# A fourth proj_w product made of seven smaller ones, and the sums of the second operand reordered, in a cross-attention block

## The chip, the cores and the metric

The kernel runs on one core of one Trainium2 chip. The metric is the device time of one execution in microseconds (us). The core has five engines that matter here, each with a queue of its own that it works through in order: TensorE (PE in the profile, its weight loads are PEld), VectorE (DVE), ScalarE (ACT), GpSimd (POOL) and SyncE (SP). In this kernel nearly all data transfers (DMAs) are issued by SP, so a transfer that has to wait also holds up those behind it in SP's queue.

## What is computed

The reference is one transformer block with cross-attention. What matters here is its last part, the MLP on the attention result `hidden` (8 sequences of 256 tokens with 512 features, taken two sequences at a time):

```python
y = layer_norm(hidden, ln2_w, ln2_b)
y = jax.nn.gelu(y @ fc_w + fc_b, approximate=True)   # 512 -> 2048
y = y @ proj_w + proj_b                              # 2048 -> 512
return residual + y
```

All of it is float32. Each float32 matmul stands as two MATMUL records in the profile.

## The kernel before

**Staging.** Four groups (g = 0 to 3) of 512 tokens each go through attention first (until about 350 us of the span) and then, one after another, through the MLP. In the MLP of a group, seven `product` calls make the 512-to-2048 part (k = 0 to 6; each is itself seven small products of four 128-column matmuls), then GELU runs on ACT, and then the 2048-to-512 part follows, which is what the change touches.

**Strassen's seven products.** The 2048-to-512 part multiplies h (512 tokens by 2048) by proj_w (2048 by 512), both cut into 2 by 2 blocks. Winograd's form of Strassen's scheme needs seven block products instead of eight, at the price of sums of blocks. The sums of h are called s1 to s4 and those of proj_w t1, t2, t4; the seven products are (11, 11), (s3, 12), (12, 21), (s2, t2), (s1, t1), (s4, 22) and (22, t4), in the kernel's order. `A_SUMS` and `B_SUMS` hold the four sums of each side; within a table each sum after the first needs an earlier one.

**Plain or deep.** `proj` makes one such product with 16 matmuls of 256 columns. From group 1 on (`deep = g > 0`) three of the seven, (s2, t2), (s1, t1) and (s4, 22), are made by `deep_proj` instead: Strassen once more, so seven products of four 128-column matmuls (28 in all). Each of the seven is one call of `sub`. Between them ACT copies and DVE adds the partial results (x1, x2, x3 and the four quarters of r); `deep_proj` also takes small lists of other work (`others`) that it puts into DVE's queue between its own adds. `h_blocks` gives the four h-side sums of one deep product as pieces on DVE; `p2_sums` makes the four proj_w-side sums of one deep product on DVE.

**The store of the proj_w sums.** The proj_w-side sums of a deep product (three blocks of 128 by 512, 768 KB) live in a buffer `p2` with two places (0 and 3). In the kernel before, T1 (t1) holds place 3 for good; T2 (t2) and B22 (22) share place 0. So B22's sums are made once, in group 1, and stored to DRAM (`p2_dram`, L1175); then T2's sums are made in the same place and stored as well; and in each later use `p2_load` (L1188) brings back the one that is needed. Who writes a place waits for the store or the matmuls that still read it.

**The order.** There is no scheduler: `manual_schedule` keeps each engine's instructions in the order in which the program gives them. Around the change this order is written out by hand. The generator `p2_late` makes B22's and T2's sums in group 1: `product` takes one step of it (`next(p2_rest)`) after the first small product of each k, so the sums stand in DVE's queue between the adds that TensorE needs (`add` at L1122 reads a PSUM bank, and the bank is free for TensorE only after that).

**What sits at the end of a group.** In group 0, which makes all seven products plainly, DVE also makes the t sums of proj_w (`some_pw`), T1's sums (`p2_sums("t1")`), the four sums of the next group's y (`y_sums`) and their second-level sums (`split_y`, L307); the adds into the result tile `resm` (`o_add`) stand between them. In groups 1 to 3 DVE makes, in this order: s3 and s2 of h, `u1` from the first product's bank, the pieces of (s2, t2), s1 of h, the pieces of (s1, t1); then the adds of the deep products. POOL makes s4 of h (in place in h12) once (12, 21) has been read. In groups 1 and 2 `turn_next` puts four transposes of the next group's tokens, two at a time, between the products on TensorE.

Of the kernel before, what the change touches and what calls it, by code (L numbers as in the profile page):

```python
# [10 lines left out]
F32 = mybir.dt.float32  # L11
# [5 lines left out]
P = 128  # L17
# [5 lines left out]
def tile_xattn_block(  # L23
# [299 lines left out]
    with ExitStack() as att:  # L323
# [282 lines left out]
        def by_tiles(row):  # L606
            return row[:, None, :].to_broadcast([P, 2, S])
# [352 lines left out]
        g = 1  # L960
# [34 lines left out]
        def run(pieces):  # L995
            for p in pieces:
                p()
# [103 lines left out]
    with ExitStack() as mlp:  # L1101
# [19 lines left out]
        def add(eng, to, a, b, op=ALU.add):  # L1121
            eng.tensor_tensor(to, a, b, op)  # L1122
# [4 lines left out]
        def load_pw(*which):  # L1127
            for n in which:
                f, d = (int(n[0]) - 1) * HF, (int(n[1]) - 1) * HD2
                nc.sync.dma_start(  # L1130
                    pw[n], proj_w.rearrange("(c p) n -> p c n", p=P)[:, f : f + HF, d : d + HD2]
                )
# [16 lines left out]

        p2, p2_at = [], {"t2": 0, "22": 0, "t1": 3}
        p2_dram = {n: tc.dram_tile([P, 3 * S * 2], F32, name=f"p2_dram_{n}") for n in ("t2", "22")}

        def p2_place(n):
            if not p2:
# [13 lines left out]
        def p2_sums(n):  # L1170
            x = pw_blocks(n)
            for i in range(4):
                sum_up(V, x, B_SUMS, i)
                if i == 3 and n != "t1":
                    nc.sync.dma_start(p2_dram[n], p2_place(n))  # L1175
                yield

        def p2_late():

            for n in ("22", "t2"):  # L1180
                for i, _ in enumerate(p2_sums(n)):
                    if n == "t2" or i:
                        yield

        p2_rest = p2_late()

# [10 lines left out]
        for g in range(NG):  # L1197
# [18 lines left out]
            def sum_h(which, q, eng=GP):  # L1216

                x = {n: h[n][:, :, 2 * q : 2 * q + 2, :] for n in h}
                to, a, b, op = {
                    "s3": ("s3", "11", "21", ALU.subtract),  # L1220
                    "s2": ("21", "22", "s3", ALU.subtract),
                    "s1": ("11", "21", "11", ALU.add),
                    "s4": ("12", "12", "21", ALU.subtract),
                }[which]
                add(eng, x[to], x[a], x[b], op)
# [29 lines left out]
            def some_gelus(n=3):  # L1255
                for f in gelus[:n]:
                    f()
                del gelus[:n]
# [17 lines left out]
            def product(k, *sums):  # L1276


                wt, yn = w2[g, k], QI[FC_ORDER[k][1]]
                bank = {}  # L1280

                def y_of(n):
                    if n in QUARTERS:
                        return ys[g].t[:, yn, int(n[0]) - 1, ts(int(n[1]) - 1, P)]
                    return y2s[g][:, ("t1", "t2", "t4").index(n), yn, :]

                def sub(n, w, b, first, last):
                    if first:
                        bank[n] = bank_of(n, f"pf{n}_{k}").rearrange("p i (j s) -> p (i j) s", j=2)
                    for m in range(HF // 2):  # L1290
                        mm(
                            bank[n][:, m, :],
                            wt[:, QI[w], ts(m, P)],
                            y_of(b),
                            first and m == 0,
                            last,
                        )

                def u(n):
                    return us(n, f"u{n}_{k}").rearrange("p i (j s) -> p (i j) s", j=2)  # L1300

                def made(cd, n, x):
                    some_gelus()
                    if k in (3, 4) and cd != "22":
                        norm_piece()
                    if sums[0][1] is None:
                        add(V, block(sums[0][0], cd), bank[n], x)
                        return

                    r = h["s3"][:, parts[0] % 4 // 2, parts[0] % 2 * HF // 2 :][:, : HF // 2]  # L1310
                    parts[0] += 1
                    add(V, r, bank[n], x)
                    for to, base in sums:
                        add(GP, block(to, cd), block(base, cd), r)

                sub(1, "11", "11", True, False)
                u1 = u(1)
                nc.scalar.copy(u1, bank[1])  # L1318
                if g == 1:
                    next(p2_rest)  # L1320
                sub(6, "s2", "t2", True, True)
                u2 = u(2)
                add(V, u2, bank[6], u1)
                some_gelus()
                sub(7, "s3", "12", True, False)
                u3 = u(3)
                add(V, u3, bank[7], u2)
                some_gelus()
                sub(5, "21", "t1", True, False)
                made("22", 5, u3)  # L1330
                sub(1, "12", "21", False, True)
                some_gelus()
                for to, base in sums:
                    if base:
                        add(V, block(to, "11"), bank[1], block(base, "11"))
                    else:
                        nc.scalar.copy(block(to, "11"), bank[1])
                sub(7, "22", "t4", False, True)
                made("21", 7, u2)
                sub(5, "s4", "22", False, True)  # L1340
                made("12", 5, u2)
                load_w2(w2_place[g, k])
# [13 lines left out]
            product(4, ("22", "12"), ("21", "21"))  # L1356
            if g == 0:
                load_pw("21")
            product(5, ("21", "21"))
            norm_piece()  # L1360
            gelu("21", 0)
# [18 lines left out]
            def proj(bank, a, w, first, last, tiles=(0, 1)):  # L1380
                for i in tiles:
                    for p in range(HF):
                        mm(
                            bank[:, i, :] if last_7 is None or i == 0 or bank is not last_7[0] else last_7[1],
                            h[a][:, i, p, :],
                            pw[w][:, p, :],
                            first and p == 0 and (i == 0 or last_7 is not None and bank is last_7[0]),
                            last and p == HF - 1,
                        )
# [11 lines left out]
            def o_add(eng, b, k, x):  # L1401
                o = out_quarter(b, k)
                add(eng, o, x, o)

            u1, u2, u3 = (us(n, f"v{n}") for n in (1, 2, 3))
            proj(bank[1], "11", "11", True, False)
            add(V, u1, bank[1], by_tiles(projb[:, HD2:]))
            some_gelus(HF)
            normalise_next()
            if deep:  # L1410
# [4 lines left out]
            def free(i):  # L1415

                return h["s3"][:, i // 2, i % 2 * HF // 2 :][:, : HF // 2]
# [48 lines left out]
            def as_tiles(r):  # L1466

                return r.rearrange("p c s -> p (c s)").rearrange("p (i s) -> p i s", i=2)
# [3 lines left out]
                run(pieces)  # L1472
            for q in range(NQF):
                sum_h("s1", q, V if deep else GP)
            proj(bank[7], "s3", "12", True, False)
            if deep:
                x_s1, pieces = h_blocks("11", free(0), free(1), free(2))
                run(pieces)
            turn_next(0)
            turn_next(1)  # L1480
            some_pw(4)
            proj(bank[1], "12", "21", False, True)
            o_add(V, 0, 0, bank[1])
            for q in range(NQF):
                sum_h("s4", q)
            turn_next(2)
# [22 lines left out]
            if deep:  # L1509
                x_s4, pieces = h_blocks("12", hsum[:, 0], hsum[:, 1], hsum[:, 3])  # L1510
                run(pieces[:1])
                deep_proj(
                    x_s1, "t1", free(3), pieces[1:2], pieces[2:3], pieces[3:], y_sums[:1], y_sums[1:2]
                )
                for b in range(2):
                    o_add(GP, b, 1, as_tiles(free(3)))
                add_us()
                deep_proj(x_s4, "22", hsum[:, 4], y_sums[2:3], y_sums[3:])
                if g + 1 < NG:
                    p2_load("t2")  # L1520
                o_add(V if g + 1 == NG else GP, 0, 1, as_tiles(hsum[:, 4]))
            else:
                add_us()
                some_pw(4)
                proj(bank[5], "11", "t1", True, True)
                o_add(V, 0, 1, bank[5])
                o_add(V, 1, 1, bank[5])
                for _ in p2_sums("t1"):
                    pass
                run(y_sums)  # L1530
                bank[3] = bank_of(1, "py3")
                proj(bank[3], "12", "22", True, True)
                o_add(V, 0, 1, bank[3])
# [56 lines left out]
```

## Time and profile before

| what | us |
|---|---|
| median of 3 runs (730.57 to 732.4) | 731.34 |
| the profiled execution's own time | 733.88 |
| its span, first to last instruction | 732.1 |
| TensorE busy in the span | 719.0 |
| DVE busy | 488.5 |
| POOL busy | 474.6 |
| ACT busy | 326.4 |
| group 1, from its first product to the GELU part | 52.33 |
| the same in groups 2 and 3, each | 43.77 |

TensorE is busy for 98% of the span, so the table is read from TensorE: a change gains what it takes out of TensorE's work or out of its few idle stretches, and loses what makes TensorE wait. Times within the execution are in us from the start of the span. In group 1 the last part runs from 496.89 to 545.69, in group 2 from 589.46 to 638.27, in group 3 from 682.04 to the end.

### The profile page before, as it was taken

Reading aid. Unit: us, or ns where it says so; the run is one execution under the profiler, and the core shown is the slowest. Engines: PE = TensorE matmul, PEld = TensorE weight load, DVE = VectorE, ACT = ScalarE, POOL = GpSimd, SP = SyncE. Lnnn points to the kernel's source line nnn. Section 1 sums busy time; section 2 is a strip of 40 time slices with the busy share of each in tenths; the row PEclk is TensorE's granted clock in tenths of the full one; section 3 lists DMA queues with packets and bytes.
Section 4 is the critical chain, followed back from the end, with each engine's and each line's share of the span. In section 5 each row is a group of like instructions: output and inputs, shape, how many; then the busy total and the mean of one; then the engine's idle time right before and its main releaser. Section 6 shows DMA issues by size and latency. Waiting matters only on the chain.

```text
span 732.1 us, 14659 instructions
## 1 busy us (share of the span) xinstructions
PE 719.0 (98%) x5325; PEld 633.5 (87%) x5325; DVE 488.5 (67%) x1177; ACT 326.4 (45%) x922; POOL 474.6 (65%) x423
## 2 busy tenths in 40 slices
PE   8999999999999999999999999699999999999998
PEld 7888777887888778777999889699999999999997
DVE  2676765675557557879588587589566894667852
ACT  2268688767777778871226200207103061030500
POOL 3758699987786999876569940475244752437423
PEclk9999999999999999999999999899999999999999
DMA  9515646687648775932899304966127951266011
GB/s 297 174 66 170 247 159 225 197 308 258 218 142 294 273 254 212 357 103 87 290 407 369 141 1 166 351 232 216 44 101 296 333 190 44 84 251 227 1 45 57
DMA packets 76392, 144.37 MB, mean 197 GB/s; under 512 B 7028, under 2 KB 45216, under 8 KB 73632
## 3 DMA queue, kind: packets, MB, share of 16 engines
q1 hardware_dynamic: 76064, 143.42, 55.9%
q8 instruction: 42, 0.69, 0.4%
q14 instruction: 30, 0.25, 0.1%
q0 software_dynamic: 256, 0.02, 0.0%
HBM read 108.29 MB, written 35.13 MB: 196 GB/s over the span
## 4 chain that ended last, share of the span: by engine, by line
PE 93%; DMA 2%; ACT 1%; DVE 1%; issue 1%; POOL 1%; SPq 0%; DVEq 0%; ACTq 0%; POOLq 0%
PE pf L1119 22%; PE py L1119 17%; PE ppt L699 8%; PE pv L441 7%; PE pqT L441 7%; PE po L441 6%; PE pd_t L1119 5%; PE pkT L441 5%; PE s L646 5%; PE av L715 4%; PE pd L1119 3%; PE pkT L538 2%; DMA p_dram<-p 2%; PE pxt L274 1%; PE pyt L274 1%
## 5 line engine op out<-in xcount | busy, mean ns | idle before, releaser
L1119 PE MATMUL pf<-y,w 128*128 128x128 f32 x1568 | 178.4, 277 | 5.9 <-DVE u L1122 5.9
L1119 PEld LDWEIGHTS pf<-y,w 128*128 128x128 f32 x1568 | 178.0, 194 | 6.4 <-DVE u L1122 6.1
L1122 POOL TENSOR_TENSOR h<-h,hs 128x512 f32<-128x512 f32 x88 | 113.5, 1312 | 104.1 <-DVE hs L1122 103.7
L688 POOL TENSOR_TENSOR pr<-pr,rsum 128x512 f32<-128x512 f32 x128 | 129.5, 1044 | 35.2 <-DVE rsum L686 23.4
L674 ACT ACTIVATE pr<-pr,nmax 128x256 f32<-128x256 f32 x256 | 127.6, 502 | 35.5 <-DVE nmax L664 35.3
L664 DVE CUSTOM_DVE_ANT_0 pr<-s,mb 128x256 f32<-128x256 f32 x256 | 93.5, 413 | 39.4 <-PE s L646 27.2
L1318 ACT COPY u<-pf 128x512 f32<-128x512 f32 x28 | 16.4, 585 | 173.0 <-PE pf L1119 173.0
L699 PEld LDWEIGHTS ppt<-ident,pr 128*128 128x128 f32 x512 | 57.3, 140 | 14.9 <-issue 5.6
L699 PE MATMUL ppt<-ident,pr 128*128 128x128 f32 x512 | 68.8, 276 | 0.3
L1119 PE MATMUL py<-pw,h 128*128 128x256 f32 x288 | 63.6, 379 | 0.0
L1119 PEld LDWEIGHTS py<-pw,h 128*128 128x128 f32 x288 | 54.2, 190 | 7.1
L1122 DVE TENSOR_TENSOR hs<-pf,u 128x512 f32<-128x512 f32 x72 | 49.5, 688 | 12.8 <-PE pf L1119 11.7
L1262 ACT ACTIVATE h<-h,cols 128x256 f32<-128x256 f32 x128 | 52.0, 495 | 11.6 <-POOL h L1122 11.6
L1122 DVE TENSOR_TENSOR u<-pf,u 128x512 f32<-128x512 f32 x56 | 38.7, 691 | 25.0 <-PE pf L1119 21.2
L704 ACT COPY pt<-ppt 128x512 f32<-128x512 f32 x96 | 51.7, 573 | 7.1 <-PE ppt L699 7.1
L441 PE MATMUL pv<-vw,ctxT 128*128 128x256 f32 x224 | 52.4, 380 | 0.0
L1122 POOL TENSOR_TENSOR h<-h,h 128x512 f32<-128x512 f32 x20 | 26.5, 1358 | 39.1 <-PE py L1119 39.1
L441 PE MATMUL pqT<-xnT,qw 128*128 128x256 f32 x224 | 51.0, 379 | 0.0
L674 ACT ACTIVATION_READ_ACCUMULATOR pr<-pr,nmax 128x1 f32 x256 | 48.8, 191 | 0.0
L441 PEld LDWEIGHTS pqT<-xnT,qw 128*128 128x128 f32 x224 | 41.4, 190 | 5.0
L441 PEld LDWEIGHTS pv<-vw,ctxT 128*128 128x128 f32 x224 | 41.0, 190 | 5.4 <-issue 0.3
L1119 PE MATMUL py<-pw_t,h 128*128 128x256 f32 x192 | 42.3, 379 | 0.0
(195 smaller groups left out, 1222.3 us busy)
## 6 DMA issues: line engine op xcount, KB each, us to landing
w<-w_dram SPq DMA_DIRECT2D x16, 1792.0 KB, 9.3
w<-in_L_xattn_fc_w_dram SPq DMA_DIRECT2D x36, 256.0 KB, 5.3
w<-w_dram SPq DMA_DIRECT2D x12, 768.0 KB, 7.2
ctx<-in_ctx_dram SPq DMA_DIRECT2D x16, 256.0 KB, 5.3
x<-in_x_dram SPq DMA_DIRECT2D x16, 256.0 KB, 4.9
v_dram<-st_v SPq DMA_DIRECT2D x16, 256.0 KB, 2.3
v<-v_dram SPq DMA_DIRECT2D x16, 256.0 KB, 5.0
resx<-in_x_dram SPq DMA_DIRECT2D x16, 256.0 KB, 4.1
```

The source lines that it names most:

```text
L441: nc.tensor.matmul(bank[n][:, i, :], l[:, c, ts(i, P)], r[:, c, :], start=first and i == 0 and c == 0, stop=last and c == HC - 1, skip_gro ...
L646: nc.tensor.matmul(banks[j][:, i, :], qT[j * HD : (j + 1) * HD, b * S + i * P : b * S + (i + 1) * P], kT[j * HD : (j + 1) * HD, b * SK : ( ...
L664: nc.vector.tensor_tensor_reduce(pr[:, j, i, :], banks[j][:, i, :], mbias[g][1][:, b, :], scale=-SCALE, scalar=FLT_MAX, op0=ALU.add, op1=A ...
L674: nc.scalar.activation(pr[:, j, i, :], pr[:, j, i, :], AF.Exp, bias=nmax[:, j, i : i + 1], scale=-1.0, accum_out=sums[:, j, i : i + 1],)
L688: nc.gpsimd.tensor_tensor(pr[:, j], pr[:, j], rsum[:, j, :, None].to_broadcast([P, NQ, SK]), ALU.mult,)
L699: nc.tensor.transpose(ps[:, kc, ts(i, P)], probs[n][:, j, i, ts(kc, P)], ident)
L704: nc.scalar.copy(pt, ps)
L715: nc.tensor.matmul(av[j * HD : (j + 1) * HD, :], vs[g, hg][:, b * NK + kc, ts(j, HD)], pts[n, j][:, kc, :], start=(kc == 0), stop=(kc == N ...
L1119: nc.tensor.matmul(ps, lhsT, rhs, start=first, stop=last, skip_group_check=True)
L1122: eng.tensor_tensor(to, a, b, op)
L1262: nc.scalar.activation(h[n][:, :, p, :], h[n][:, :, p, :], AF.Gelu_apprx_tanh, bias=col(c_fcb, half * HF + p), scale=1.0,)
L1318: nc.scalar.copy(u1, bank[1])
```

## The change

Five things change, all in the MLP:

1. The product (12, 21) is made by `deep_proj` in groups 1 to 3. Its h-side pieces go into the four quarters of the `hs3` tile (`free(0)` to `free(3)`), and the result into `hsum[:, 4]`. The first product's bank is added to the result directly after `u1` is made, and the pieces of (s1, t1) are made after the new product instead of before it.
2. B21 gets proj_w-side sums like the other three. They are made in group 0 in place 3, stored, and T1's sums then take the same place 3 and are stored too. So place 3 is shared now: B21's sums are loaded in group 1 after product 4 and, in groups 1 and 2, after (s1, t1); T1's are loaded after (12, 21) in groups 1 to 3. That adds two stores and six loads of 768 KB.
3. `p2_late` has two empty steps between the store of B22's sums and T2's first sum, which so falls into product 5 instead of product 3. T2's last two sums and its store come out of an eighth step, ahead of (s3, 12) in the program.
4. In (s4, 22) the last two of the four `y_sums` stand one place later in DVE's queue each.
5. The result of (s4, 22) goes to `free(0)` instead of `hsum[:, 4]`.

```diff
-        p2, p2_at = [], {"t2": 0, "22": 0, "t1": 3}
-        p2_dram = {... for n in ("t2", "22")}
+        p2, p2_at = [], {"t2": 0, "22": 0, "t1": 3, "21": 3}
+        p2_dram = {... for n in p2_at}
...
-                if i == 3 and n != "t1":
+                if i == 3:
                     nc.sync.dma_start(p2_dram[n], p2_place(n))
                 yield
...
         def p2_late():
-            for n in ("22", "t2"):
-                for i, _ in enumerate(p2_sums(n)):
-                    if n == "t2" or i:
-                        yield
+            for i, _ in enumerate(p2_sums("22")):
+                if i:
+                    yield
+            yield
+            yield
+            for i, _ in enumerate(p2_sums("t2")):
+                if i < 2:
+                    yield
+            yield
...
             if g == 0:
                 load_pw("21")
+            if g == 1:
+                p2_load("21")
             product(5, ("21", "21"))
...
-            proj(bank[1], "11", "11", True, False)
+            proj(bank[1], "11", "11", True, deep)
             add(V, u1, bank[1], by_tiles(projb[:, HD2:]))
+            if deep:
+                o_add(V, 0, 0, bank[1])
...
                 sum_h("s1", q, V if deep else GP)
+            if g == 1:
+                next(p2_rest)
             proj(bank[7], "s3", "12", True, False)
-            if deep:
-                x_s1, pieces = h_blocks("11", free(0), free(1), free(2))
-                run(pieces)
             turn_next(0)
             turn_next(1)
             some_pw(4)
-            proj(bank[1], "12", "21", False, True)
-            o_add(V, 0, 0, bank[1])
+            if deep:
+                x_12, pieces = h_blocks("12", *(free(i) for i in range(4)))
+                run(pieces[:2])
+                deep_proj(x_12, "21", hsum[:, 4], pieces[2:3], pieces[3:])
+                p2_load("t1")
+                o_add(V, 0, 0, as_tiles(hsum[:, 4]))
+                x_s1, pieces = h_blocks("11", free(0), free(1), free(2))
+                run(pieces)
+            else:
+                proj(bank[1], "12", "21", False, True)
+                o_add(V, 0, 0, bank[1])
             for q in range(NQF):
                 sum_h("s4", q)
...
                     x_s1, "t1", free(3), pieces[1:2], pieces[2:3], pieces[3:], y_sums[:1], y_sums[1:2]
                 )
+                if g + 1 < NG:
+                    p2_load("21")
...
-                deep_proj(x_s4, "22", hsum[:, 4], y_sums[2:3], y_sums[3:])
+                deep_proj(x_s4, "22", free(0), (), (), y_sums[2:3], y_sums[3:])
                 if g + 1 < NG:
                     p2_load("t2")
-                o_add(V if g + 1 == NG else GP, 0, 1, as_tiles(hsum[:, 4]))
+                o_add(V if g + 1 == NG else GP, 0, 1, as_tiles(free(0)))
             else:
                 add_us()
                 some_pw(4)
+                for _ in p2_sums("21"):
+                    pass
                 proj(bank[5], "11", "t1", True, True)
```

More of the change, by code (lines that the diff above doesn't have):

```diff
@@ L1147, in tile_xattn_block @@
         pw_sums = sum_pw()
-        p2, p2_at = [], {"t2": 0, "22": 0, "t1": 3}
-        p2_dram = {n: tc.dram_tile([P, 3 * S * 2], F32, name=f"p2_dram_{n}") for n in ("t2", "22")}
+        p2, p2_at = [], {"t2": 0, "22": 0, "t1": 3, "21": 3}
+        p2_dram = {n: tc.dram_tile([P, 3 * S * 2], F32, name=f"p2_dram_{n}") for n in p2_at}
         def p2_place(n):
```

## Prediction

> **What bounds the kernel now.** The first view is the busy time of each engine: PE is busy 719.0 of 732.1 us (98%), so only PE's own work and its few idle stretches can move the time. The second is the list of who waited: PE's longest wait is 5.9 us for DVE (u, L1122), then 0.8 us in two (pd for hsum). The third is PE by stretches, from a group's first product to its GELU part, in groups 1, 2 and 3:
>
> ```profile
> core 0: us, PE busy (x), PEclk, DMA share, GB/s
> 444.56:496.89 52.33, 46.41 (x394) 0.93 0.73 263
> 545.69:589.46 43.77, 43.77 (x394) 1.00 0.84 300
> 638.27:682.04 43.77, 43.77 (x394) 1.00 0.56 205
> ```
>
> The same 394 records take 8.56 us more in group 1: 5.92 of it idle, the rest at a lower granted clock (0.93). The chain of waits says where it begins:
>
> ```profile
> 457.95 1.02 DVE p L219
> 458.99 12.71 DMA p_dram<-p
> 471.69 0.02 issue
> 471.72 0.03 DVE p L219
> ...
> 473.86 23.19 PE pf L1119 x184
> ```
>
> DVE ended B22's last sum at 458.97; the store took 12.71 us among big loads; T2's first sum wants the same place and stood at the head of DVE's queue for 7.4 us, and the adds that free PE's banks stood behind it. The clock by microsecond shows the second part of the price:
>
> ```profile
> 471.00:472.00 1.00, 0.00 (x0) 0.81 1.02 436
> 472.00:473.00 1.00, 0.00 (x0) 0.50 1.04 444
> ...
> 477.00:478.00 1.00, 1.00 (x7) 0.50 0.00 0
> 478.00:479.00 1.00, 1.00 (x9) 0.77 0.28 57
> ```
>
> PE stopped at 467.95; the clock halved at about 471.6 and came back at about 478.5, 4.6 us after PE had resumed at 473.86.
>
> **T2's sums moved: -8.56 us.** T2's first sum goes from product 3 to product 5, which starts at 444.56 + 5 x 6.25 = 475.8; the store lands at 471.7, so 4 us to spare. DVE's place in product 3 becomes free, and group 1 should take 43.77 like the others. What is late next: product 5's weights, issued at 463.51, landed 12.5 us later (476.0), 0.2 us after 475.8; so far the stall hid that. With 0.1 for the restart I take +0.3 (0 to 1.5). Product 4's weights (issued 457.25, 9.3 us) land at 466.6 against 469.6.
>
> **The matmuls: -1.98 us.** (12, 21) as plain product is 16 matmuls, 6.91 us in the chain. The existing deep ones take 12.51 us for 112 records, 0.893 us per small product; seven are 6.25. Three groups gain 0.66 each, if fed. Set against each other instruction by instruction, the two programs differ on DVE by 34 more (four sums in group 0; per group four pieces, five adds of partial results, one more add into the result), on ACT by two copies per group, on POOL by none. ACT's copies are hidden: ACT is idle from 507.6 to 511.3 and waits for PE from then on; late, they would delay x2 by 0.27 each. POOL's s4 sums begin near the end of the new product, as they do near the end of the plain one; they are needed at (s4, 22), over 8 us later.
>
> **Feeding it: +7.94 us.** Here the order on DVE against PE decides. Group 1, DVE and then PE:
>
> ```profile
> 506.87 0.68 DVE L1122 TENSOR_TENSOR v<-py,projb 128x512 f32<-128x512 f32 x1
> 507.47 0.68 DVE L1122 TENSOR_TENSOR hsum<-h 128x512 f32<-128x512 f32 x1
> ...
> 512.53 0.68 DVE L1122 TENSOR_TENSOR hs<-h 128x512 f32<-128x512 f32 x1
> 513.31 0.69 DVE L1122 TENSOR_TENSOR hs<-h,hs 128x512 f32<-128x512 f32 x1
> ```
>
> ```profile
> 503.80 7.07 PE L1119 MATMUL py<-pw,hs 128*128 128x256 f32 x32
> 510.70 1.04 PE L274 MATMUL pyt<-ident,hm 128*128 128x128 f32 x8
> 511.57 7.07 PE L1119 MATMUL py<-pw,h 128*128 128x256 f32 x32
> ```
>
> The new product's first small one (11, 11) needs no sum and runs from 511.57 to 512.46. Its second needs the second piece (s2). On DVE that piece stands where the second `hs` of (s1, t1) stands now (513.31 to 514.00), but behind one more add (`o_add` of the first bank, 0.61 from issue to issue, as at 444.82) and, in group 1, behind two T2 sums (0.60 each). So it ends at 514.00 + 1.81 = 515.81, and with 0.04 for the handover PE stands for 3.39 us. Group 2: piece now ends 606.08, + 0.61 + 0.04 = 606.73, against PE at 604.15 + 0.89 = 605.04: 1.69. Group 3 has no transposes to cover it: 698.66 + 0.65 = 699.31 against 695.86 + 0.89 = 696.75: 2.56. Each restart costs 0.1 more (the small product after the hsum wait took 1.00 instead of 0.89). Sum 7.64 + 0.30. Nothing hides this: the GELU and POOL's adds are done by then, and POOL is idle, so DVE runs at its 0.6 us rate.
>
> **Inside it: +1.02 and +0.5 us.** The fourth small product needs the s1 piece, which DVE takes only after adding x2. By the spacing after the hsum stall (bank added 1.20 after the small product's start, next DVE start 0.2 later, 0.68 long) it is ready 2.13 us after the second small one starts; PE wants it at 1.89. With the restart 0.34, three times. The pieces of (s1, t1) now stand between this product and the adds of (s2, t2): `o_add` and four pieces, some 3.8 us with POOL's s4 sums alongside (DVE's adds took 1.4 instead of 0.6 us while POOL added, at 498.84). In groups 1 and 2 two transposes cover it; in group 3 x3 of (s2, t2) comes some 0.4 us late: +0.5 (0 to 1). The loads of T1's sums have 9 us and took 4.1 to 4.4.
>
> **Group 0's end: +1.5 us.** T1's sums now wait for the store of B21's. The DVE rows there:
>
> ```profile
> 432.22 0.68 DVE L219 TENSOR_TENSOR p<-pw_t 128x512 f32<-128x512 f32 x1
> ...
> 437.85 0.69 DVE L1122 TENSOR_TENSOR resm<-py,resm 128x512 f32<-128x512 f32 x1 [0.42 <-PE py L1119]
> ...
> 441.58 1.08 DVE L307 TENSOR_TENSOR y<-y,y 128x896 f32<-128x896 f32 x1
> 444.82 0.69 DVE L1122 TENSOR_TENSOR resm<-py,resm 128x512 f32<-128x512 f32 x1 [2.16 <-PE py L1119]
> ```
>
> B21's four sums (2.6 us, as T1's) start at 430.5 and end at 433.1. Hardly a transfer runs there; 768 KB stores of other tiles took 4.0 (cw), 4.2, 5.0 and 6.5 us (w), the two of p_dram 8.6 and 12.7 among loads. I take 4.0, for the quiet. T1's sums start at 437.15 instead of 432.22; behind them stand the y sums, an add, `split_y` and the add that frees bank 7. That add would end at 437.15 + 2.53 + 2.6 + 0.61 + 4.1 + 0.69 = 447.7; PE wants the bank at 444.56 + 2 x 0.893 = 446.35: 1.4 and a restart. Each us more of the store is one more of waiting: +2.5 at 5.0, +4.0 at 6.5, +6.1 at 8.6; 0 if it took 2.6, near the 2.2 of a 256 KB store.
>
> **y sums later: -1.32 us.** From the start of (s2, t2) to that of (22, t4) groups 1 and 2 need 19.42 and 19.43 us, group 3, without y sums, 18.76. The y sums stood ahead of the add that the seventh small product waits for; moved behind, DVE still ends `split_y` before the next group's second small product. Writing to the hs3 tile takes no DVE or PE time: its last readers are a product earlier. The other five loads and one store go into SP stretches with no transfers (GB/s near 0 from 506 to 524); what hides them is that quiet, and one that came late would cost its lateness.
>
> **Sum.** -8.56 + 0.3 - 1.98 + 7.94 + 1.02 + 0.5 + 1.5 - 1.32 = -0.60 us. The profiled execution took 733.88 (span 732.1, 1.8 around it), so 733.3; the median of the runs is 2.5 lower, and from it the forecast is 731.34 - 0.6 = 730.7.
>
> **A rule against it.** The trace has one long stop: the clock halved 3.65 us after PE stopped, and that cost 8.56 - 5.92 = 2.64. My largest new stop is 3.39, so I price no clock loss; no row shows a stop of 1 to 5 us, so each may cost 0 to 2.64. The Trainium skill ("TensorE: Matmul & The Clock Gate", section "HAM oscillation — how this bites in real kernels") says that idle gaps over about 3.4 us throttle the clock to half, by a free-running window; the 3.65 agrees. By that rule taken to the letter 3.39 stays just under and the sum stands at 730.7; with the gap a little longer, or nearly a window counted as one, the sum would be 733.3.
>
> **Rivals.**
> - *The clock falls in the new stops* (slower). PE stands 3.4 and 2.6 us before the new product's second small one in groups 1 and 3; if a mostly idle stretch is enough, each costs 2.64: 730.7 + 5.3 = 736.0. It decides from about 2.6 us of idleness. For: the clock did fall here. Against: it took 3.65 us. 0.13.
> - *The covers hold* (faster). The store of B21 is covered, product 5's weights come in time, group 3's x3 too: -1.5 - 0.3 - 0.5, so 728.4, less if the second pieces come sooner than the rows say. For: each is a margin of under 1.5 us. Against: DVE's queue is in strict order and its spacings come from rows. 0.27.
> - *B21's store takes 8.6 us* as T2's did among loads: PE stands 6 us at group 1's start, + 4.6 and a clock fall of 2.6: 737.9. Against: hardly a transfer runs from 426 to 438. 0.08.
> - *It doesn't do what it says*: B22's store still lands after T2's first sum in product 5, the stall stays: 739.3. It would have to land 4 us later. 0.02.
>
> **Chances.** Forecast 0.50 (own range 729.1 to 733.5). About 0.3% (2.2 us) is what a measurement can tell from no change; so faster 0.27, same 0.50, slower 0.23. The range leaves out the two last rivals and the far end of the second: 727.5 to 736.0.
>
> **What would show it.** In the changed profile: group 1's seven products at 44 to 45 us with clock 1.00 and no p_dram wait on the chain (T2 step); PE waits for DVE hs of about 3.4, 1.7 and 2.6 us at pd (feeding), with clock 1.00 through them (no fall); a DVE wait for p_dram near 434 and PE waiting 1.4 us in group 1's first product; 18.8 us from (s2, t2) to (22, t4) in groups 1 and 2. The forecast is wrong if the pd waits are under 1 us, or the clock drops beside them.

## The result and the profile after

The changed kernel takes **733.8 us** (median of 20 runs, 732.06 to 738.58), the kernel before 731.77 (20 runs beside them, 730.57 to 733.71). The ratio is 1.0031 with a 95% interval of 1.0018 to 1.0043: 2.0 us slower, where the forecast was 0.6 faster. The profiled execution took 734.65 with a span of 732.9.

PE by stretches in the changed kernel: first the seven products of group 1, then the last parts of groups 1, 2 and 3. The columns are length, PE busy with its records, granted clock, DMA share and GB/s.

```profile
442.90:487.98 45.08, 44.35 (x394) 1.00 0.85 327
...
487.98:540.43 52.45, 49.46 (x338) 0.97 0.37 132
584.21:634.47 50.26, 48.25 (x339) 1.00 0.34 122
678.24:732.90 54.66, 48.06 (x322) 0.97 0.14 49
```

Group 1's products have fallen from 52.33 to 45.08, at full clock: the stop for T2's first sum is gone. All three last parts have grown, and in groups 1 and 3 the clock there is 0.97.

| stretch | before | after | forecast of the difference | measured |
|---|---|---|---|---|
| group 1, products | 52.33 | 45.08 | -6.76 | -7.25 |
| group 1, last part | 48.80 | 52.45 | +2.51 | +3.65 |
| group 2, last part | 48.81 | 50.26 | +0.81 | +1.45 |
| group 3, last part to the end | 50.06 | 54.66 | +2.84 | +4.60 |
| sum | | | -0.60 | +2.45 |

The two profiled spans differ by only 0.8 us, because the profiled execution of the kernel before reached the first of these stretches 1.66 us later (at 444.56 against 442.90); a second profile of the same kernel reached it at 441.64.

The list of who waited has a new wait at its head (us in total, times, longest); the old one, 5.9 us for DVE's u, is no longer there:

```profile
PE pd L1119 <- DVE hs L1122: 7.2, 4, 3.0
```

The new product's small products in group 1, on PE's timeline (start, length; x8 is one small product; the bracket gives the idle time before it and its releaser):

```profile
502.67 1.06 PE L1119 MATMUL pd<-pw,h 128*128 128x128 f32 x8
506.71 1.16 PE L1119 MATMUL pd<-p,hs 128*128 128x128 f32 x8 [2.99 <-DVE hs L1122]
507.70 1.62 PE L1119 MATMUL pd<-pw,hs 128*128 128x128 f32 x8
509.11 1.95 PE L1119 MATMUL pd<-p,hs 128*128 128x128 f32 x8
510.85 1.34 PE L1119 MATMUL pd<-pw,h 128*128 128x128 f32 x8
```

A fed small product starts 0.893 after the one before. Here the second starts 4.04 after the first (the stop: 3.15 lost), and then come starts 0.99, 1.41, 1.74 and 1.18 apart (the next one is at 512.03): the last three have no listed wait and are slow. The clock says why (half-microsecond slices; PEclk is the number after the records):

```profile
506.50:507.00 0.50, 0.29 (x2) 1.00 0.94 393
...
507.50:508.00 0.50, 0.50 (x7) 1.00 0.94 369
508.00:508.50 0.50, 0.50 (x5) 0.53 0.01 0
...
511.00:511.50 0.50, 0.50 (x5) 0.56 0.00 0
```

The clock halved at 508.03 (a slice at 0.53 is full speed for 0.03 us), 1.3 us after PE had resumed, and came back at 511.44. The stops before the same small product in groups 2 and 3 are shorter:

```profile
601.52 1.16 PE L1119 MATMUL pd<-p,hs 128*128 128x128 f32 x8 [1.57 <-DVE hs L1122]
...
695.54 1.91 PE L1119 MATMUL pd<-p,hs 128*128 128x128 f32 x8 [2.44 <-DVE hs L1122]
```

Group 3's clock falls too, from 695.76 to 699.17; group 2, with the shortest stop, keeps its clock.

```profile
695.50:696.00 0.50, 0.46 (x3) 0.76 0.00 0
...
699.00:699.50 0.50, 0.50 (x5) 0.83 0.00 0
```

### The profile page after: what moved, and what is told of

It reads as the page before. It is cut to its first block, busy times and chain, and to the rows that moved or that the text cites. A ratio compares the mean times of both kernels' runs of the same rounds, so it can differ in the third digit from the quotient of the medians.

```text
span 732.9 us, 14878 instructions
## 1 busy us (share of the span) xinstructions
PE 718.0 (98%) x5397; PEld 634.3 (87%) x5397; DVE 509.9 (70%) x1211; ACT 327.7 (45%) x928; POOL 477.4 (65%) x423
## 4 chain that ended last, share of the span: by engine, by line
PE 77%; DVE 9%; DMA 6%; issue 4%; ACT 2%; POOL 1%; SPq 0%; DVEq 0%; POOLq 0%
PE pf L1119 19%; PE ppt L699 8%; PE pv L441 7%; PE pqT L441 7%; PE py L1119 5%; PE pd L1119 5%; PE po L441 5%; PE pkT L441 5%; PE s L646 5%; PE av L715 4%; PE pd_t L1119 4%; PE pkT L538 2%; DVE h L1122 2%; DMA pw<-in_L_xattn_proj_w_dram 2%; DMA w<-w_dram 2%
## 5 line engine op out<-in xcount | busy, mean ns | idle before, releaser
L1119 PEld LDWEIGHTS pf<-y,w 128*128 128x128 f32 x1568 | 175.9, 192 | 1.3 <-DVE resm L1122 0.7
L1119 PE MATMUL pf<-y,w 128*128 128x128 f32 x1568 | 176.3, 275 | 0.7 <-DVE resm L1122 0.5
L1122 POOL TENSOR_TENSOR h<-h,h 128x512 f32<-128x512 f32 x20 | 28.0, 1425 | 43.7 <-DVE hs L1122 42.8
L1119 PE MATMUL py<-pw,h 128*128 128x256 f32 x192 | 42.4, 379 | 0.0
L1119 PEld LDWEIGHTS py<-pw_t,h 128*128 128x128 f32 x192 | 36.2, 190 | 4.7
```

The costliest lines, as they stand in the source:

```text
L1119: nc.tensor.matmul(ps, lhsT, rhs, start=first, stop=last, skip_group_check=True)
```

## The experiments

All were run beside the kernel before, which took 731.93 us (first four) and 732.08 (last four). The question of the first four: is the rest of the price the clock, and is the gain of T2's move what I took it to be?

**The kernel before again, with a new profile.** No edit.

> The kernel before, unchanged, for its granted clock run by run. Clock theory (the missing 2.6 us are lost because the clock falls in the changed kernel's new stops of PE): nothing special is expected, its stop of 5.9 us costs a clock fall in nearly every run, mean clock about 0.995 as in the profile. Rival (the profiled execution of the kernel before was dear, 733.9 against a median of 731.8, because it paid a clock fall that most of its runs don't, so that moving T2's sums gains only about 6 us in the median instead of 8.56): mean clocks of 0.998 to 1.0 in most runs, with times of 731 to 732 there and 733 to 734 at 0.995.

732.27 us (730.85 to 732.7, 11 runs); PE's stop is 5.83 us long and the clock is between 0.993 and 0.995 in every run. So the kernel before pays for its stop each time, and the rival falls. This profile's span is 729.1 against 732.1 of the one that I predicted from.

**T2's move alone.** In the kernel before, only the new `p2_late`, and its last step ahead of (s3, 12):

```diff
+            if g == 1:
+                next(p2_rest)
             proj(bank[7], "s3", "12", True, False)
```

> Of the change only T2's sums moved behind B22's store; the product (12, 21) stays plain. Clock theory: the whole 8.56 minus 0.3 for product 5's weights is gained in the median too: 731.8 - 8.3 = 723.5. Rival: only the idle time and its restart, 6.0 minus 0.3: 726.1. Both: group 1's seven products at about 44 us, clock 1.00, PE waits for DVE under 1.5 us in all.

723.14 us (722.87 to 724.58), ratio 0.9883 (0.9869 to 0.9896), clock 0.999 to 1.000: 8.8 us gained. Group 1's products in its profile, against 52.33 at a clock of 0.93:

```profile
442.30:486.33 44.03, 44.03 (x393) 1.00 0.83 313
```

Both the idle time and the clock's share come back. It follows that the rest of the change costs 733.8 - 731.77 + 8.8 = 10.8 us.

**PE kept busy in the new stops.** The changed kernel, with transposes into a scratch bank in front of the second small product of (12, 21):

```diff
+                if fill:
+                    warm_ps = ps_m.tile([P, G], F32, tag="mm", name=f"keep_{g}")
+                    for k in range(fill):
+                        nc.tensor.transpose(warm_ps[:, ts(k % NT, P)], ident, ident)
                 sub(1, "s2", "t2", True, True)
...
-                deep_proj(x_12, "21", hsum[:, 4], pieces[2:3], pieces[3:])
+                deep_proj(x_12, "21", hsum[:, 4], pieces[2:3], pieces[3:], fill=(0, 13, 7, 11)[g])
```

> The changed kernel with transposes of the identity that nobody reads put on PE between the first and the second small product of (12, 21), 13, 7 and 11 of them in groups 1 to 3 (2.9, 1.6 and 2.5 us), so that PE is busy while it waits for the second piece; the waiting itself stays. Clock theory: the clock stays at 1.00 there, each fall that is avoided gives 1.6 us, and with two falls in most runs the median drops by 2 to 3.3: 730.5 to 731.8. Rival: the stops are what costs, not the clock: 733.8, within 0.5.

733.02 us (732.09 to 734.76), ratio 1.0015 (1.0007 to 1.0024), clock 0.998 to 1.000: between the two expectations. PE's waits in its group 3:

```profile
694.02 1.16 PE L1119 MATMUL pd<-p,hs 128*128 128x128 f32 x8 [1.24 <-DVE hs L1122]
696.32 1.13 PE L1119 MATMUL pd<-p,hs 128*128 128x128 f32 x8 [0.25 <-DVE hs L1122]
705.67 1.16 PE L1119 MATMUL pd_t<-p,h 128*128 128x128 f32 x8 [1.07 <-DVE p L1122]
```

The profile's clock is 1.00 throughout the last parts, so the falls came from PE's idleness in the stops. But two waits that the slow clock had covered appear: 0.25 for the s1 piece (0 in the changed kernel's group 3) and 1.07 for x2 or x3 of (s2, t2) (0.68 there). The last part of group 1 went from 52.45 to 51.69 and of group 3 from 54.66 to 53.89: by these two stretches a fall costs 0.77 net, not the 1.6 that its slow small products lose. The transposes took 0.11 each, so 13 of them filled only 1.4 us of group 1's stop.

**The pieces first.** The changed kernel with the pieces of s2 ahead of the s1 sums and of T2's last sums, which go between the new product's own adds:

```diff
-            for q in range(NQF):
-                sum_h("s1", q, V if deep else GP)
-            if g == 1:
-                next(p2_rest)
+            s1_sums = [lambda q=q: sum_h("s1", q, V if deep else GP) for q in range(NQF)]
+            if not deep:
+                run(s1_sums)
...
-                deep_proj(x_12, "21", hsum[:, 4], pieces[2:3], pieces[3:])
+                deep_proj(x_12, "21", hsum[:, 4], pieces[2:3], pieces[3:], s1_sums[:2], s1_sums[2:])
+                if g == 1:
+                    next(p2_rest)
...
-                x_s1, pieces = h_blocks("11", free(0), free(1), free(2))
-                run(pieces)
+                x_s1, s1_pieces = h_blocks("11", free(0), free(1), free(2))
...
-                deep_proj(x_s2, "t2", hsum[:, 4])
+                deep_proj(x_s2, "t2", hsum[:, 4], *([f] for f in s1_pieces))
```

> The changed kernel with DVE's order altered: the first two pieces of (12, 21) ahead of the four s1 sums and of T2's last sums; these follow inside the new product, and the pieces of (s1, t1) inside (s2, t2). Both theories: the stops of 3.15, 1.73 and 2.60 us before the second small product shrink to 0, 0 and about 0.2, and the late x2 and x3 of (s2, t2) go. Clock theory: 7.3 of stops, 1.2 of late adds and 2.8 of clock: 733.8 - 11.3 = 722.5. Rival: without the clock's share: 725.3.

727.96 us (727.7 to 729.96), ratio 0.9954 (0.994 to 0.9967), clock 1.000. The long stops are gone, down to 0.25 each, and yet the kernel is 4.8 us behind T2's move alone. On DVE in group 1:

```profile
506.11 2.65 DVE L1122 TENSOR_TENSOR h<-h,h 128x512 f32<-128x512 f32 x2
...
508.89 3.23 DVE L1122 TENSOR_TENSOR h<-h,h 128x512 f32<-128x512 f32 x2
```

Two s1 sums took 2.65 and 3.23 us, because POOL added s4 at the same time (from 504.76, four adds in 6.82); in the changed kernel, ahead of POOL's, four took 2.49. PE then waited 1.77 for T2's last sums (512.25 to 513.45) and 1.17 for the load of T1's, and in group 3 1.15 for an add of a partial result (hsum). Both expectations (722.5 and 725.3) fell: the sums moved away from one stop came back as others. The Trainium skill ("SBUF — State Buffer", section "SBUF: two separate sides") says that a VectorE operation with two SBUF inputs and a GpSimd operation take turns at a shared port; that agrees in kind, and the price here is 1.3 to 1.6 us for an add instead of 0.6.

The question of the last four: how much of the price goes with the product itself, and does a better order exist?

**T2's move and the y sums, without the product.** T2's move alone, and:

```diff
-                deep_proj(x_s4, "22", hsum[:, 4], y_sums[2:3], y_sums[3:])
+                deep_proj(x_s4, "22", free(0), (), (), y_sums[2:3], y_sums[3:])
...
-                o_add(V if g + 1 == NG else GP, 0, 1, as_tiles(hsum[:, 4]))
+                o_add(V if g + 1 == NG else GP, 0, 1, as_tiles(free(0)))
```

> The run with T2's sums alone moved, and with it the parts of the change on the y sums and on where the result of (s4, 22) goes; (12, 21) stays plain. My step: 0.66 in each of groups 1 and 2, so 1.3 below that run's 723.1: 721.8, and 18.8 us from (s2, t2) to (22, t4) in groups 1 and 2. Rival (DVE catches the y sums up elsewhere, at the next group's first product): 723.1.

**722.15 us** (722.0 to 722.18), ratio 0.9861 (0.9841 to 0.9881). This version beats both kernels. Group 1's products take 44.03, and its last parts 48.14, 48.14 and 50.05; those of groups 1 and 2 stand against 48.81 with T2's move alone: the y sums are worth 0.67 twice, as forecast. Through all of group 2, from its products at 534.83 to its last one at 619.83, the chain of waits is PE and nothing else:

```profile
534.83 43.77 PE pf L1119 x392
578.60 13.82 PE py L1119 x64
...
601.07 12.51 PE pd_t L1119 x112
613.58 6.25 PE pd L1119 x56
619.83 6.91 PE py L1119 x32
```

**The fourth product without its h-side sums.** The changed kernel; the four sums are left out and stale data stands in for them:

```diff
-                x_12, pieces = h_blocks("12", *(free(i) for i in range(4)))
-                run(pieces[:2])
-                deep_proj(x_12, "21", hsum[:, 4], pieces[2:3], pieces[3:])
+                x_12, pieces = h_blocks("12", *(hsum[:, i] for i in range(4)))
+                deep_proj(x_12, "21", hsum[:, 4])
```

> The changed kernel without the four h-side sums of (12, 21): its small products read sums of another product, so this part of the result is not what it should be; the matmuls, the partial adds, loads and stores stay. If the pieces on DVE are what the new product costs, its stops go (3.15, 1.73 and 2.60 us, 0.3 in the middle, the clock falls and the late adds of (s2, t2)), and it gains its 0.66 per group against plain: 721.8 of the run before this one, less 2.0, plus 1.1 at group 0's end: 720.9. Rival (the seven small products are dearer than 6.25 us even when fed, or the loads and partial adds cost): 722 to 725 with 6.5 to 7.5 us for the product.

723.48 us (722.69 to 723.9), ratio 0.9879 (0.9861 to 0.9896): the rival's 722 to 725, by its second condition, since the seven small products take 6.25 us where they are fed. By stretches (group 1's products and group 2's last part):

```profile
442.47:487.62 45.15, 44.33 (x393) 1.00 0.86 328
...
579.87:627.44 47.57, 47.57 (x339) 1.00 0.35 126
```

In group 2 PE never waits, and the seven small products gain 0.57 (47.57 against 48.14): the gain of the matmuls exists. But group 1's products still pay 1.1 (45.15 against 44.03) for B21's store and the late weights, and PE waits for adds of partial results, 0.63 in group 1 (behind T2's last sums, 1.76 each beside POOL) and 0.68 in group 3. Its slowest run is faster than any of the changed kernel, its fastest slower than any without the product. Part of that is of this edit's own making: with nothing on DVE reading h12 any more, POOL starts s4 at 503.17 instead of 509.03 and slows T2's last sums (0.68 each in the changed kernel), and the wait behind them costs 0.9 of the 1.3 us that this version lies above the one without the product. So even with its h-side sums free the product would gain nothing clear here.

**The product with T2 where it was.** The changed kernel with the old `p2_late`, no eighth step.

> The changed kernel with T2's sums put back to product 3. If the parts add up, the stall behind the store is back at 8.6 less 0.3: 733.8 + 8.3 = 742.1. Rival (part of that gain depends on the other parts, because stops in one place give transfers time elsewhere): 739 to 741.

740.97 us (739.87 to 741.13), ratio 1.0116 (1.0097 to 1.0134). That is 8.9 over the kernel before, 6.9 more than the changed kernel's 2.0: T2's move is worth 6.9 beside the product and 8.8 alone, the rival's side. With T2's last two sums out of its way the piece of s2 came 0.9 us sooner in group 1, and group 3 kept its clock (53.89 against 54.66), which together make 1.7 of the 1.9 between them. PE's stops in groups 1 and 3, and then the last parts around them with their clock:

```profile
512.68 1.53 PE L1119 MATMUL pd<-p,hs 128*128 128x128 f32 x8 [2.08 <-DVE hs L1122]
...
701.53 1.16 PE L1119 MATMUL pd<-p,hs 128*128 128x128 f32 x8 [2.45 <-DVE hs L1122]
```

```profile
494.85:546.39 51.54, 49.46 (x338) 0.97 0.35 135
...
684.21:738.10 53.89, 46.66 (x322) 1.00 0.14 50
```

Two falls begin in this execution, one in the old stall (468.94) and one at the stop of 2.08 us (513.32 to 516.72):

```profile
468.50:469.00 0.50, 0.00 (x0) 0.94 1.05 446
```

```profile
513.00:514.00 1.00, 1.00 (x8) 0.66 0.00 0
...
516.00:517.00 1.00, 1.00 (x8) 0.64 0.00 0
```

The stop of 2.08 us had its clock halved and the stop of 2.45 did not: length alone does not decide.

**Another order.** The pieces first (`s1_sums` and `s1_pieces` are lists as in the run above), T2's sums two to a step inside the products, and the s1 sums between the adds of (s2, t2):

```diff
-                if i < 2:
+                if i % 2:
                     yield
-            yield
...
-                deep_proj(x_s2, "t2", hsum[:, 4])
+                deep_proj(x_s2, "t2", hsum[:, 4], s1_sums[:2], s1_sums[2:], s1_pieces[:1], s1_pieces[1:3], s1_pieces[3:])
```

> The run with the pieces first, with DVE's work spread further: T2's sums two to a step in products 5 and 6, the s1 sums and the pieces of (s1, t1) inside (s2, t2), nothing but its own pieces inside (12, 21). If DVE's order is the whole trouble, the 1.8, 1.2 and 1.2 us that PE still waited in (s2, t2) go, and (12, 21) gains its 0.66 per group: 728.0 less 5 to 6: 722 to 723, at or just under the run that moves T2's sums alone. Rival (DVE has too much work between a group's GELU and (s1, t1), however it is ordered): above 724.5.

726.95 us (726.11 to 727.35), ratio 0.9926 (0.991 to 0.9941), clock 1.000. T2's sums pushed DVE past PE within group 1's products:

```profile
480.08 6.52 PE L1119 MATMUL pf<-y,w 128*128 128x128 f32 x56 [0.81 <-DVE u L1122]
487.17 2.05 PE L1119 MATMUL pf<-y,w 128*128 128x128 f32 x16 [0.57 <-DVE u L1122]
```

Those products take 47.30 against 44.03 without the fourth product. And group 2, which has no T2 sums, still takes 48.41 against 48.14: waits of 0.25 and 0.17, with what PE loses around them, take 0.84 (48.41 against the fed 47.57). The time lies on the rival's side (above 724.5), but most of the excess is T2's sums inside the products (47.30 against 44.03), not the place that the rival names. No order that was tried gains anything from the product.

## Why the prediction was wrong

**T2's sums moved (-8.56, with +0.3 for product 5's weights) and y sums (-1.32): right.** Together -9.58; the version with these two alone measured 722.15 - 732.08 = -9.93. Its group 1 products took 0.26 more than 43.77, lost where product 5 begins; in the changed kernel the listed wait for these weights is 0.25.

**The matmuls (-1.98): right to a seventh.** 0.57 a group in the one fed case, forecast 0.66.

**Feeding it: the stops were right.** Listed waits of 2.99, 1.57 and 2.44. Against a fed start, the second small product lost 3.15, 1.74 and 2.60, where 3.39, 1.69 and 2.56 were forecast. The restarts cost 0.1, as taken.

**A rule against it: the step that failed.** "My largest new stop is 3.39, so I price no clock loss." The clock fell in groups 1 and 3 after stops of 3.0 and 2.4 us, and the next small products lost 0.52 + 0.85 + 0.29 = 1.66 (group 1) and 0.82 + 0.81 + 0.12 = 1.75 (group 3). The forecast had 0.34 in these places for the s1 wait, and in group 3 the restart's 0.1 as well; so +1.3 in each group. I had read the 3.65 us from stop to fall in the old stall as the shortest stop that costs a fall. It is one delay, and says nothing of shorter stops. (Nor is it so that no row showed a stop of 1 to 5 us: the list of waits has one of 1.4 at the very start; it has no bearing on these.)

The rival that named this had the mechanism, at 0.13; its price of 5.3 was too high. The 2.64 was carried over from a fall that lasted 6.84 us (471.62 to 478.46), and these last 3.41 each. Net, a fall costs 0.77, since the s1 wait and late partial results hide under the slow clock. Nor does every execution have two: of the 20 runs the four with a mean clock of at least 0.999 took 732.06 to 732.71, the eight at 0.997 to 0.998 had a median of 733.6, the five at 0.995 one of 734.25, and the three at 0.993 took 735.67 to 738.58. A fall of 3.41 us at half speed takes 1.7 / 732 = 0.0023 off the mean clock, so by the clock these are runs with none, one, two and three falls. In the median the falls are worth 733.8 - 732.3 = 1.5 us: the four runs without one (median 732.3) lie within the forecast's own range of 729.1 to 733.5, 0.5 over the kernel before instead of 0.6 under it. The other 1.1 comes from the terms that follow.

**Inside it: too low.** The s1 wait, seen clean in group 2, cost 0.49 with its restart instead of 0.34. The late x2 or x3 of (s2, t2) was forecast for group 3 alone, 0.5, because "in groups 1 and 2 two transposes cover it". They do not quite: 0.46 lost in group 2 (0.35 and a restart), 0.95 in group 3, and 0.43 in group 1 once the clock is held. On DVE in group 2, `o_add` and the pieces ran from 608.07 to 612.5 (4.4 us); I had taken 3.8.

**Group 0's end (+1.5): too high.** B21's store, with hardly a transfer beside it, took 3.22 us instead of my 4.0:

```profile
431.48 3.22 DMA p_dram<-p
```

DVE waited 2.07, PE 0.49 in group 1's first product:

```profile
445.33 29.79 PE L1119 MATMUL pf<-y,w 128*128 128x128 f32 x264 [0.49 <-DVE resm L1122]
475.37 12.77 PE L1119 MATMUL pf<-y,w 128*128 128x128 f32 x112 [0.25 <-DMA w<-w_dram]
```

With its restart, and the weights later than without the product, group 1's products cost 45.08 - 44.03 = 1.05 over the version without the fourth product, where 1.5 was forecast.

**The sum.** Set against the version without the product, stretch by stretch, the product costs 1.05 + 4.31 + 2.12 + 4.61 = 12.1 us in the profiles; my terms for it give -1.98 + 7.94 + 1.02 + 0.5 + 1.5 = 9.0. The miss of 3.1 is the slow small products (+2.6), the late partial results in groups 2 and 3 (+0.9) and the s1 wait in group 2 (+0.15), less group 0's end (-0.45) and the stops (-0.15). The slow small products stand here with all that they lose; half of it would have been lost to the waits under them anyway, as the version that kept the clock shows.

What stays open: the version that kept the clock is at 733.02, 1.1 above the kernel before, and the changed kernel's four runs without a fall (median 732.3) only 0.5. What the transposes cost and what the other parts of the program vary by were not told apart.

## What to carry to other kernels

Before an engine's saving is counted, count what feeds it: here 0.6 us of TensorE per product asked for ten more DVE adds and two ACT copies per group, and the sums behind the first small product alone took back 1.7 to 3.2. Two edits in one change can hide each other, so the one that gains should be timed alone: T2's move with the y sums was worth 1.4%, and the product ate it. When a stop is added, price a clock fall by the share of a window that it leaves idle and the window's length, not by the one long stop that the old trace shows.

## What the runs showed of the chip

**The clock's windows.** Falls last 3.41 us each (508.03 to 511.44, 695.76 to 699.17), and the two falls begin 187.73 us apart, 55.0 times 3.413. In the version with T2 where it was they begin at 468.94 and 513.32, 44.38 apart, 13.0 times that. The fall in the old stall lasted twice as long, 6.84. So the clock looks as if set by a free-running grid. If each fall comes at the end of the window that was judged, PE had been idle in 61% of it in group 1 (504.62 to 506.71) and in 71% in group 3; group 2's stop of 1.57 fills at most 39% of one, and there was no fall. The version with T2 where it was narrows this. Its stop of 2.08 us lies whole in the window that ends at 513.32 (61%), and the clock fell. Its stop of 2.45, from 699.08 to 701.53, is cut by the window's end at 513.32 + 55 x 3.413 = 701.04; 57% of one window was idle, and the clock held. By this reading the bound lies between 57% and 61%; no run was made to test it.

The Trainium skill ("TensorE: Matmul & The Clock Gate", section "HAM oscillation — how this bites in real kernels") puts the bite at idle gaps over about 3.4 us. Here gaps of 2.1 to 3.0 us were enough; the measurement decides.

**A restart.** The first small product after a stop took 0.96 to 1.00 instead of 0.893, after stops from 0.2 to 3 us alike. A listed wait is shorter than what it costs: the 0.19 of group 2's (s2, t2) cost 0.46, since a listed wait begins at the modelled end of a small product (1.06 after its start, where the next fed one starts after 0.893), and the restart comes on top.
